# Summing attention weights over keys: accumulating DMAs in place of TensorE products and VectorE pair sums, with new scheduling priorities

## The chip, the cores and the metric

One core of one Trainium2 chip. The metric is device microseconds of one execution of the whole program. Every run quoted here was in the fast state. TensorE's granted clock is given as a share of full speed.

## The reference, cut to what matters

Sixteen graphs of 1024 nodes with 256 features share one sparse adjacency matrix. Each passes three graph-attention layers and then one layer of masked 8-head attention with a feed-forward part, all in fp32. The change concerns the attention layer:

```python
x, adj                                            # (16, 1024, 256), (1024, 1024)
for layer in (L0, L1, L2):                        # graph attention with 4, 1 and 1 heads
    x = x + layer(relu(layernorm(x)), adj, W, a)
h = relu(layernorm(x))
q, k, v = split(h @ w_qkv)                        # 8 heads of 32
scores = einsum('fnhd,fmhd->fhnm', q, k) / sqrt(32)
attn = softmax(where(adj > 0, scores, -1e9), -1)  # <- numerators and denominators
t = einsum('fhnm,fmhd->fnhd', attn, v)
h = layernorm(h + t); h = layernorm(h + ffn(h))
out = x + h                                       # the last residual; its x is loaded into the tile xr
```

## The kernel before

The kernel doesn't emit instructions where they are written. It records them, with a duration for each, and a list scheduler puts them into one fixed order per engine. Several batches are in flight, each an offset stream of priorities: a piece of work has as its key the batch number plus a position inside the stage, and of the work that is ready the smallest key goes first.

```python
class Record:
    def schedule(self):
        ...
            if x.key is None:
                x.key = base + span * x.pos / max(total, 1e-9)
        ...
            if x.moved:                               # a DMA: x.moved us of transfer
                queue[e] = max(at + 0.2, queue[e]) + x.moved
                x.pass_on = queue[e] + LANDING - (at + us)
```

`e` is the issuing engine: the model has one line of transfers for SyncE, another for GpSimd, and each moves at its own full pace. That will matter.

One attention layer has 32 steps: 2 groups of heads x 2 halves of the queries x 8 blocks of keys. I call the eight steps of one group and half a run. A step makes two tiles of masked exponentials (`pas`, 128 x 1024 each), multiplies them with the values on TensorE (a "quad": four column-tiled matmuls, one for each head, for two tiles), and needs their sum over keys, the denominator, by a quad against ones.

```python
def paired(g, hf):
    return g == 1 or hf == 1          # three runs of four
...
pe((1 + both) * 0.855, lambda: value(m, both), ...)   # both: also weights x ones
if not both and jt % 2:               # a quad on the sum of two steps
    pe(0.855, lambda: quad(accs[g, hf][1], ..., lambda r: ones, ...), ...)
...                                   # (cut: scores, exps, mask multiplies)
if paired(g, hf) and jt % 2:
    sums[n] = [r_sums.new() for _ in range(2)]
    for ss, p0, p1 in zip(sums[n], pas[n - 1], pas[n]):
        dve(tt_us(2 * HALF), lambda: nc.vector.tensor_add(ss.t, p0.t, p1.t), [ss], [p0, p1])
```

So one run in four multiplies every step by ones (8 quads), and three runs add pairs on VectorE and multiply those (4 quads each). The end of a batch matters too, because its transfers are what will suffer; `xr` has two buffers:

```python
def back(hf):
    for it in (hf * TH, hf * TH + 2):
        xr = r_xr.new()
        dma(1.15, lambda: nc.sync.dma_start(xr.t, x3.t[:, it : it + 2, :]), [xr(0), xr(1)], [x3(hf)])
        dve(tt_us(2 * C), lambda: nc.vector.tensor_add(xr.t, xr.t, rows["c2"]...), ...)
        ...                           # (cut: transposes, layer norm, scale, shift)
        dma(0.65, lambda: nc.sync.dma_start(out[b]...[:, it : it + 2, :], xr.t), [], [xr(0), xr(1)])
```

Of the kernel before, what the change touches and what calls it, by code (L numbers as in the profile page):

```python
# [17 lines left out]
ALU = mybir.AluOpType  # L18
# [96 lines left out]


class Record:

# [5 lines left out]

    def stream(self, base, span):


        self.streams.append([base, span, 0.0])

# [32 lines left out]
    def schedule(self):  # L162
        for n, x in enumerate(self.work):
            x.n = n
            base, span, total = x.stream
            if x.key is None:
                x.key = base + span * x.pos / max(total, 1e-9)
            x.left = len(x.before)
            for y in x.before:
                y.after.append(x)  # L170
# [43 lines left out]
        while True:  # L214
# [13 lines left out]
            us = x.us  # L228
# [24 lines left out]
LANDING = 2.5  # L253
BIAS = 0.516

# [18 lines left out]
def tt_us(n):  # L274
    return (n / 0.96 + 73) / 1000
# [17 lines left out]
def direct(ctx, tc, flag, x, adj, gat_w, gat_a, w_qkv, ln1_g, ln1_b, ln2_g, ln2_b, w1, b1, w2, b2, out):  # L293


    nc = tc.nc
# [7 lines left out]

    GATS = (0.0, 0.388), (0.388, 0.271), (0.659, 0.201)
    VALUES, STEPS, FEED = (1.132, 0.099), (1.231, 0.63), (2.355, 0.252)

# [84 lines left out]
    def dve(us, emit, w, r):  # L392
        rec.add("dve", us, emit, w, r)
# [196 lines left out]
    def setup():  # L590
        rec.stream(-3.0, 1.0)
        prepare(0)
        rec.stream(-0.9, 0.1)
        for it in range(NT):
            neighbours(it)
        rec.stream(-0.5, 0.3)
        prepare(1)
        prepare(2)
        dma(
            3.2,  # L600
            lambda: nc.sync.dma_start(wqkv_sb, w_qkv.rearrange("(t p) d -> p t d", p=P)),
            [b_qkv],
            [],
        )

        def load_feed():
            nc.sync.dma_start(w1_sb, w1.rearrange("(t p) d -> p t d", p=P))
            nc.sync.dma_start(w2_sb, w2.rearrange("(t p) d -> p t d", p=P))
            for n, ap in (("b1", b1), ("b2", b2), ("g1", ln1_g), ("c1", ln1_b)):
                nc.sync.dma_start(cols[n], ap.rearrange("(t p) -> p t", p=P))  # L610
            for n, ap in (("g2", ln2_g), ("c2", ln2_b)):
                nc.sync.dma_start(rows[n][:, 0, :], rows_on_all(ap, C))

        dma(5.0, load_feed, [b_feed], [], us=3.6)
# [346 lines left out]
    def attention(b, xt, b_mv, b_rstd):  # L961
        rec.stream(b + VALUES[0], VALUES[1])
        mv, rstd = b_mv.t, b_rstd.t
# [127 lines left out]

        def quad(ac, jt, of_head, columns, first, last):
            for r in range(HG):
# [7 lines left out]

        def value(n, both):

            g, hf, jt = steps[n]
            for ac in accs[g, hf][: 1 + both]:
                quad(
                    ac,
                    jt,
                    lambda r: pas[n][r // 2].t[:, r % 2, :],
                    lambda r: (  # L1110
                        ones
                        if ac is accs[g, hf][1]
                        else va.t[:, jt, (g * HG + r) * D3 : (g * HG + r + 1) * D3]
                    ),
                    jt == 0,
                    jt == NT - 1,
                )

        def paired(g, hf):

            return g == 1 or hf == 1

        rec.stream(b + STEPS[0], STEPS[1])
        GROUP = 2
        LAG = 2
        for n in range(len(steps) + LAG):
            m = n - LAG
            if m >= 0:
                g, hf, jt = steps[m]
                if jt == 0:  # L1130
                    accs[g, hf] = [r_bank.new(), r_bank.new()]
                both = not paired(g, hf)
                pe(
                    (1 + both) * 0.855,
                    lambda: value(m, both),
                    accs[g, hf],
                    pas[m] + [va(jt)],
                    ("col4", "col4"),
                )
                if not both and jt % 2:  # L1140
                    ss = sums[m]
                    pe(
                        0.855,
                        lambda: quad(
                            accs[g, hf][1],
                            jt,
                            lambda r: ss[r // 2].t[:, r % 2, :],
                            lambda r: ones,
                            jt == 1,
                            jt == NT - 1,  # L1150
# [56 lines left out]
            if n < len(steps):  # L1207
# [7 lines left out]
                for r0 in range(0, HG, GROUP):  # L1215
# [25 lines left out]
                    for r in range(r0, r0 + GROUP):  # L1241
# [9 lines left out]
                        if v:  # L1251
# [11 lines left out]
                            )  # L1263
                if paired(g, hf) and jt % 2:
                    sums[n] = [r_sums.new() for _ in range(2)]
                    for ss, p0, p1 in zip(sums[n], pas[n - 1], pas[n]):
                        dve(
                            tt_us(2 * HALF),
                            lambda: nc.vector.tensor_add(ss.t, p0.t, p1.t),  # L1269
                            [ss],  # L1270
                            [p0, p1],
                        )
        watch(b_rec, b_rec.t, 1)
# [178 lines left out]
    def batch(b):  # L1452
        xt, b_mv, b_rstd, x3 = Halves(r_xt), r_mv.new(), r_rstd.new(), r_x3.new()
        x_b = x[b].rearrange("(t p) c -> p t c", p=P)
        rec.stream(b, 0.0)
        for hf in range(2):
# [10 lines left out]
        for l in range(3):  # L1467
            rec.stream(b + GATS[l][0], GATS[l][1])
            gat(xt, b_mv, b_rstd, l)
# [8 lines left out]
        hn = attention(b, xt, b_mv, b_rstd)  # L1478
        rec.stream(b + FEED[0], FEED[1])
        feed(b, x3, hn)  # L1480
# [616 lines left out]
```

## Time and profile before

| | before |
|---|---|
| time, median of 4 runs | 4244.05 us (4240.61 to 4247.3) |
| TensorE / VectorE / ScalarE busy | 98% / 88% / 54% |
| DMA engines busy (the plain transfers' queue) | 22% |
| granted clock | 0.995 |
| denominator quads on TensorE | 320 (128 on weights, 192 on pair sums) |
| pair sums on VectorE | 384 |

How to read it: TensorE sets the time. The prediction below shows the lines that say so.

### The profile page before, as it was taken

To read this page: it belongs to the slowest core of one execution; us is meant where nothing else is said; L and a number is where in the kernel's file an instruction comes from. 1 tells how busy PE (TensorE), PEld (TensorE's weight loads), DVE (VectorE), ACT (ScalarE), POOL (GpSimd) and SP (SyncE) were. 2 spreads that over 40 slices of the span, in tenths; PEclk is the share of its full clock that TensorE was granted. 3 is DMA by queue.
4 is the path that set the end of the run, shared out by engine and by line. 5 is a ranking of instruction groups with operands and counts; after the bars stand their busy time and mean duration, and the time that the engine had idled before them with its cause. 6 is when DMAs were issued, how large, how long until landed. Compare 5 with 4: busy or idle time off the path is not lost.

```text
span 4234.8 us, 68471 instructions
## 1 busy us (share of the span) xinstructions
PE 4144.4 (98%) x24738; PEld 2385.9 (56%) x24738; DVE 3713.0 (88%) x6786; ACT 2307.1 (54%) x5041; POOL 351.7 (8%) x391
## 2 busy tenths in 40 slices
PE   7999999999999999999999999999999999999997
PEld 3746466564655646556464665646556465564642
DVE  7589898997989889898998989989898898988977
ACT  2445555554655645556555555656556455565564
POOL 0000010010100100001000100101001000010000
PEclk9999999999999999999999999999999999999998
DMA  3121222212222122221212222122212222212131
GB/s 103 50 66 36 76 66 66 56 46 70 68 75 53 50 66 61 81 63 56 60 48 75 66 66 56 50 66 71 76 52 60 56 60 81 64 52 60 47 82 39
DMA packets 180682, 263.82 MB, mean 62 GB/s; under 512 B 41328, under 2 KB 76400, under 8 KB 180336
## 3 DMA queue, kind: packets, MB, share of 16 engines
q1 hardware_dynamic: 180336, 259.36, 22.2%
q8 instruction: 198, 3.24, 0.3%
q14 instruction: 148, 1.21, 0.1%
HBM read 91.03 MB, written 33.95 MB: 30 GB/s over the span
## 4 chain that ended last, share of the span: by engine, by line
PE 73%; DVE 12%; ACT 7%; issue 3%; DMA 3%; POOL 2%; SPq 1%; DVEq 0%; ACTq 0%; POOLq 0%
PE bank L787 19%; PE bank L1094 12%; PE bank L861 9%; PE sc L1221 9%; PE bank L1327 5%; PE bank L871 5%; PE bank L663 4%; PE bank L460 4%; PE sc L1010 4%; DVE pa L1254 3%; DVE pt L760 2%; POOL rstd L412 2%; ACT hn L431 2%; ACT hna L431 2%; PE sc L1046 2%
## 5 line engine op out<-in xcount | busy, mean ns | idle before, releaser
L1245 ACT ACTIVATE pa<-sc 128x512 f32<-128x512 f32 x2048 | 1093.7, 608 | 610.3 <-PE sc L1221 524.7
L1254 DVE TENSOR_TENSOR pa<-pa,mask 128x1024 f32<-128x1024 f32 x1024 | 1220.2, 1215 | 48.5 <-ACT pa L1245 48.4
L760 DVE SCALAR_TENSOR_TENSOR pt<-row,e,mask 128x512 f32<-128x512 f32 x1536 | 1054.9, 744 | 90.7 <-DMA row<-rd 55.8
L787 PE MATMUL bank<-qb,pt 128*128 128x257 f32 x4096 | 940.9, 382 | 1.0 <-DVE pt L760 0.5
L787 PEld LDWEIGHTS bank<-qb,pt 128*128 128x128 f32 x4096 | 767.7, 190 | 197.5 <-ACT pa L1245 40.0
L1221 PE MATMUL sc<-qs,ks 128*128 128x512 f32 x2048 | 682.0, 446 | 2.9 <-ACT pa L1245 2.1
L1094 PE MATMUL bank<-pa,va 128*32 128x512 f32 x4096 | 533.0, 597 | 3.6 <-DVE pa L1254 3.2
L861 PE MATMUL bank<-pt,qb 128*32 128x512 f32 x4096 | 515.4, 595 | 7.3 <-DVE pt L760 6.7
L1221 PEld LDWEIGHTS sc<-qs,ks 128*128 128x128 f32 x2048 | 363.6, 188 | 237.1 <-ACT pa L1245 93.7
L1269 DVE TENSOR_TENSOR sums<-pa,pa 128x1024 f32<-128x1024 f32 x384 | 457.0, 1214 | 0.3 <-PE bank L1094 0.2
L663 PE MATMUL bank<-w_aug,hT 128*128 128x259 f32 (+1 forms) x1536 | 374.3, 388 | 4.3 <-ACT e L674 3.6
L815 ACT ACTIVATE ex<-bank,rec 128x256 f32<-128x256 f32 x256 | 122.1, 477 | 437.5 <-DVE rec L807 396.1
L663 PEld LDWEIGHTS bank<-w_aug,hT 128*128 128x128 f32 x1536 | 286.2, 191 | 74.0 <-issue 12.8
L412 POOL TENSOR_TENSOR rstd<-rstd,neg_half 128x4 f32<-128x4 f32 x160 | 203.1, 1272 | 1468.6 <-DVE rstd L409 1417.4
L861 PEld LDWEIGHTS bank<-pt,qb 128*32 128x32 f32 x4096 | 127.1, 109 | 310.0 <-issue 214.5
L871 PE MATMUL bank<-pt,e 128*32 128x512 f32 x2048 | 292.1, 592 | 0.0
L1094 PEld LDWEIGHTS bank<-pa,va 128*32 128x32 f32 x4096 | 116.2, 109 | 267.7 <-issue 208.7
L1010 PE MATMUL sc<-hTa,wqkv_sb 128*128 128x512 f32 x512 | 240.1, 596 | 4.6 <-ACT hTa L995 4.6
L431 ACT ACTIVATE hn<-xt,mv,rstd 128x256 f32<-128x256 f32 x384 | 206.3, 601 | 40.4 <-DVE mv L421 39.6
L892 ACT COPY ot<-bank 128x512 f32<-128x512 f32 x128 | 74.8, 586 | 257.7 <-PE bank L861 215.3
L1094 PE MATMUL bank<-sums,ones 128*32 128x512 f32 x1536 | 208.0, 596 | 0.8
L403 DVE BATCH_NORM_STATS2 stg<-xt 128x6 f32<-128x256 f32 x512 | 205.4, 414 | 3.2
(107 smaller groups left out, 3993.7 us busy)
## 6 DMA issues: line engine op xcount, KB each, us to landing
row<-rd SPq DMA_DIRECT2D x192, 256.0 KB
ks<-hi SPq DMA_DIRECT2D x512, 64.0 KB
ks<-lo SPq DMA_DIRECT2D x512, 64.0 KB
qs<-hi SPq DMA_DIRECT2D x512, 64.0 KB
qs<-lo SPq DMA_DIRECT2D x512, 64.0 KB
xt<-in_x_dram SPq DMA_DIRECT2D x32, 512.0 KB
x<-xt SPq DMA_DIRECT2D x32, 512.0 KB
xr<-x SPq DMA_DIRECT2D x64, 256.0 KB
```

What stands on the lines that cost most here:

```text
L431: lambda: nc.scalar.activation(dst, src, func, bias=bias, scale=scale),
L663: nc.tensor.matmul(g.t[:, : C + 3 * H], hT.t[:, ct, k * P : (k + 1) * P], w_aug[l][:, ct, :], start=ct == 0, stop=ct == CT - 1,)
L760: lambda: nc.vector.scalar_tensor_tensor(pt.t, row.t, e3[:, 2, jt // TH, h, jt % TH : jt % TH + 1], mask[:, jt, hf * HALF : (hf + 1) * HAL ...
L787: nc.tensor.matmul(g.t[:, : D + 1], pts[jt].t[:, k * P : (k + 1) * P], qb[:, jt, 0, :], start=jt == 0, stop=jt == NT - 1,)
L861: nc.tensor.matmul(g.t[u * D + d : u * D + d + D3, :], qb[:, j, h + u, d : d + D3], pts[u][j - jt].t, start=j == 0, stop=j == NT - 1,)
L871: nc.tensor.matmul(gd.t[c : c + D3, :], one(jt + k, h + u).to_broadcast([P, D3]), pts[u][k].t, start=jt == 0, stop=jt == NT - 2,)
L1010: nc.tensor.matmul(sc.t, wqkv_sb[:, ct, c0 : c0 + P], hT.t[:, ct, hf * HALF : (hf + 1) * HALF], start=ct == 0, stop=ct == CT - 1,)
L1094: nc.tensor.matmul(ac.t[r * D3 : (r + 1) * D3, :], columns(r), of_head(r), start=first, stop=last,)
L1221: nc.tensor.matmul(scs[r - r0].t, ks.t[:, r, jt * P : (jt + 1) * P].bitcast(F32R), q.t[:, r, :].bitcast(F32R), start=True, stop=True,)
L1245: lambda: nc.scalar.activation(pt.t[:, v, :], sc.t, AF.Exp, scale=1.0 / math.sqrt(D3)),
L1254: lambda: nc.vector.tensor_mul(pt.t, pt.t, mask[:, jt : jt + 1, i0 : i0 + HALF].to_broadcast([P, 2, HALF]),),
L1269: lambda: nc.vector.tensor_add(ss.t, p0.t, p1.t),
```

## The change

Intent: take work from the two fullest engines and give it to the DMA engines, which are three quarters idle. In every run VectorE adds the first two steps into a tile, six DMAs per tile add the other steps onto it, and one quad per run multiplies the result by ones. Priorities get five knots per stage in place of a straight line, an offset for ScalarE's and VectorE's work (`LEAD`) and a stronger bias against changes of TensorE's mode. The diff, cut to its core:

```diff
+def priority(x):
+    base, knots, total, lead = x.stream
+    at = x.pos / max(total, 1e-9) * (len(knots) - 1)
+    k = max(0, min(int(at), len(knots) - 2))
+    key = base + knots[k] + (knots[k + 1] - knots[k]) * (at - k)
+    return round(key - (LEAD.get(x.engine, 0.0) if lead else 0.0), 6)
...
-BIAS = 0.516
+BIAS = 0.676
+LEAD = {"act": -2.125, "dve": 1.391}
...
-    GATS = (0.0, 0.388), (0.388, 0.271), (0.659, 0.201)
-    VALUES, STEPS, FEED = (1.132, 0.099), (1.231, 0.63), (2.355, 0.252)
+    GATS = ((-0.005, 0.055, 0.156, 0.243, 0.247), ...)
+    VALUES = (1.165, 1.186, 1.197, 1.164, 1.074)
+    STEPS = (1.085, 1.251, 1.421, 1.645, 1.91)
+    FEED = (2.225, 2.388, 2.391, 2.491, 2.389)
...
+        RUN = 8
...
+                if jt % RUN == 1:
+                    sums[g, hf] = [r_sums.new() for _ in range(2)]
+                    for ss, p0, p1 in zip(sums[g, hf], pas[m - 1], pas[m]):
+                        dve(tt_us(2 * HALF), lambda: nc.vector.tensor_add(ss.t, p0.t, p1.t), [ss], [p0, p1])
+                elif jt % RUN:
+                    for ss, pt in zip(sums[g, hf], pas[m]):
+                        dma(2.8, lambda: nc.gpsimd.dma_start(ss.t, pt.t, accum_op=ALU.add),
+                            [ss], [pt], us=0.88, engine="pool")
...
-                if not both and jt % 2:
-                    ss = sums[m]
+                if jt % RUN == RUN - 1:
+                    ss = sums[g, hf]
                     pe(0.855, ...quad against ones...)
...
-                if paired(g, hf) and jt % 2:
-                    ...pair sums on VectorE...
```

More of the change, by code (lines that the diff above doesn't have):

```diff
@@ L123, in __init__, with stream @@
         self.streams = []
-    def stream(self, base, span):
-        self.streams.append([base, span, 0.0])
+    def stream(self, base, knots, lead=True):
+        self.streams.append([base, knots, 0.0, lead])
     def add(self, engine, us, emit, w=(), r=(), modes=("full", "full"), key=None, moved=0.0):
@@ L164, in schedule @@
             x.n = n
-            base, span, total = x.stream
             if x.key is None:
-                x.key = base + span * x.pos / max(total, 1e-9)
+                x.key = priority(x)
             x.left = len(x.before)
@@ L303, in direct @@
     HG = P // D3
-    GATS = (0.0, 0.388), (0.388, 0.271), (0.659, 0.201)
-    VALUES, STEPS, FEED = (1.132, 0.099), (1.231, 0.63), (2.355, 0.252)
+    GATS = (
+        (-0.005, 0.055, 0.156, 0.243, 0.247),
+        (0.285, 0.416, 0.523, 0.588, 0.743),
+        (-0.041, 0.393, 0.575, 0.619, 0.945),
+    )
+    VALUES = (1.165, 1.186, 1.197, 1.164, 1.074)
+    STEPS = (1.085, 1.251, 1.421, 1.645, 1.91)
+    FEED = (2.225, 2.388, 2.391, 2.491, 2.389)
     const = ctx.enter_context(tc.tile_pool(name="const", bufs=1))
@@ L590, in setup @@
     def setup():
-        rec.stream(-3.0, 1.0)
+        rec.stream(-3.0, (0.0, 1.0), False)
         prepare(0)
-        rec.stream(-0.9, 0.1)
+        rec.stream(-0.9, (0.0, 0.1), False)
         for it in range(NT):
             neighbours(it)
-        rec.stream(-0.5, 0.3)
+        rec.stream(-0.5, (0.0, 0.3), False)
         prepare(1)
@@ L961, in attention @@
     def attention(b, xt, b_mv, b_rstd):
-        rec.stream(b + VALUES[0], VALUES[1])
+        rec.stream(b, VALUES)
         mv, rstd = b_mv.t, b_rstd.t
@@ L1090, in attention, with quad @@
         pas, accs, sums = {}, {}, {}
-        def quad(ac, jt, of_head, columns, first, last):
+        def quad(ac, of_head, columns, first, last):
             for r in range(HG):
@@ L1100, in quad @@
                 )
-        def value(n, both):
-            g, hf, jt = steps[n]
-            for ac in accs[g, hf][: 1 + both]:
-                quad(
-                    ac,
-                    jt,
-                    lambda r: pas[n][r // 2].t[:, r % 2, :],
-                    lambda r: (
-                        ones
-                        if ac is accs[g, hf][1]
-                        else va.t[:, jt, (g * HG + r) * D3 : (g * HG + r + 1) * D3]
-                    ),
-                    jt == 0,
-                    jt == NT - 1,
-                )
-        def paired(g, hf):
-            return g == 1 or hf == 1
-        rec.stream(b + STEPS[0], STEPS[1])
+        RUN = 8
+        rec.stream(b, STEPS)
         GROUP = 2
@@ L1131, in attention @@
                     accs[g, hf] = [r_bank.new(), r_bank.new()]
-                both = not paired(g, hf)
-                pe(
-                    (1 + both) * 0.855,
-                    lambda: value(m, both),
-                    accs[g, hf],
+                if jt % RUN == 1:
+                    sums[g, hf] = [r_sums.new() for _ in range(2)]
+                    for ss, p0, p1 in zip(sums[g, hf], pas[m - 1], pas[m]):
+                        dve(
+                            tt_us(2 * HALF),
+                            lambda: nc.vector.tensor_add(ss.t, p0.t, p1.t),
+                            [ss],
+                            [p0, p1],
+                        )
+                elif jt % RUN:
+                    for ss, pt in zip(sums[g, hf], pas[m]):
+                        dma(
+                            2.8,
+                            lambda: nc.gpsimd.dma_start(ss.t, pt.t, accum_op=ALU.add),
+                            [ss],
+                            [pt],
+                            us=0.88,
+                            engine="pool",
+                        )
+                pe(
+                    0.855,
+                    lambda: quad(
+                        accs[g, hf][0],
+                        lambda r: pas[m][r // 2].t[:, r % 2, :],
+                        lambda r: va.t[:, jt, (g * HG + r) * D3 : (g * HG + r + 1) * D3],
+                        jt == 0,
+                        jt == NT - 1,
+                    ),
+                    [accs[g, hf][0]],
                     pas[m] + [va(jt)],
@@ L1145, in attention @@
                             accs[g, hf][1],
-                            jt,
                             lambda r: ss[r // 2].t[:, r % 2, :],
                             lambda r: ones,
-                            jt == 1,
+                            jt == RUN - 1,
                             jt == NT - 1,
@@ L1263, in attention @@
                             )
-                if paired(g, hf) and jt % 2:
-                    sums[n] = [r_sums.new() for _ in range(2)]
-                    for ss, p0, p1 in zip(sums[n], pas[n - 1], pas[n]):
-                        dve(
-                            tt_us(2 * HALF),
-                            lambda: nc.vector.tensor_add(ss.t, p0.t, p1.t),
-                            [ss],
-                            [p0, p1],
-                        )
         watch(b_rec, b_rec.t, 1)
@@ L1454, in batch @@
         x_b = x[b].rearrange("(t p) c -> p t c", p=P)
-        rec.stream(b, 0.0)
+        rec.stream(b, (0.0, 0.0), False)
         for hf in range(2):
@@ L1467, in batch @@
         for l in range(3):
-            rec.stream(b + GATS[l][0], GATS[l][1])
+            rec.stream(b, GATS[l])
             gat(xt, b_mv, b_rstd, l)
@@ L1478, in batch @@
         hn = attention(b, xt, b_mv, b_rstd)
-        rec.stream(b + FEED[0], FEED[1])
+        rec.stream(b, FEED)
         feed(b, x3, hn)
```

## The prediction

> **What bounds the kernel now.** I read the page's engine shares first, then busy time by stretch, then the groups of instructions, then the chain that ended last, then the DMA part and the waits.
>
> ```profile
> PE 4144.4 (98%) x24738; PEld 2385.9 (56%) x24738; DVE 3713.0 (88%) x6786; ACT 2307.1 (54%) x5041; POOL 351.7 (8%) x391
> ...
> q1 hardware_dynamic: 180336, 259.36, 22.2%
> ```
>
> TensorE is busy 98% of the span, VectorE 88%, GpSimd 8%, the DMA engines 22%. A busy share can hide waiting, so I asked for stretches (columns: window, its length, busy us and instructions of PE, PEld, DVE, ACT and POOL, then TensorE clock, DMA share, GB/s):
>
> ```profile
> 0.00:100.00 100.00, 75.83 (x522) 34.20 (x526) 81.11 (x176) 28.52 (x57) 4.62 (x12) 0.93 0.33 109
> ...
> 400.00:4000.00 3600.00, 3573.69 (x21602) 2077.61 (x21602) 3224.59 (x5886) 2003.46 (x4399) 309.14 (x336) 1.00 0.23 62
> ...
> 4100.00:4235.00 135.00, 111.65 (x490) 41.26 (x488) 109.97 (x168) 64.29 (x120) 9.21 (x9) 0.92 0.20 52
> ```
>
> From 400 to 4000 us TensorE is idle for 3600 - 3573.69 = 26 us, 0.7%. The kernel interleaves the streams of several batches, and there the schedule leaves almost nothing to take from waits: only removed TensorE time shortens it. The idle time is at the two ends. Does "busy" mean "at its pace"? The chain of waits in order of time answers (start us, us, what):
>
> ```profile
> 1536.33 1.14 PE sc L1221 x4
> 1537.47 1.85 PE bank L861 x16
> ...
> 1540.18 1.72 PE bank L861 x16
> ...
> 1542.76 3.44 PE bank L1094 x32
> ```
>
> Link follows link without a hole, and 32 instructions of L1094 take 3.44 us. Such a quad (four matmuls on four column groups) is 8 instructions, so a quad advances the chain by 0.86 us. That is the pace I use; the 1.04 us that a lone quad shows as busy in the timeline includes an end that overlaps its successor. The groups that the change touches (busy us, mean ns of one | idle before):
>
> ```profile
> L1254 DVE TENSOR_TENSOR pa<-pa,mask 128x1024 f32<-128x1024 f32 x1024 | 1220.2, 1215 | 48.5 <-ACT pa L1245 48.4
> ...
> L1269 DVE TENSOR_TENSOR sums<-pa,pa 128x1024 f32<-128x1024 f32 x384 | 457.0, 1214 | 0.3 <-PE bank L1094 0.2
> ...
> L1094 PE MATMUL bank<-sums,ones 128*32 128x512 f32 x1536 | 208.0, 596 | 0.8
> ```
>
> VectorE adds pairs of weight tiles (384 adds of 1.214 us) and TensorE sums over keys by quads against ones: 1536 / 8 = 192 on pair sums. A further group, the weights against ones directly, has 1024 instructions in the full list of groups: 128 quads, from the quarter of the attention that isn't paired.
>
> **What the Trainium skill says.** (1) "DMA: Bandwidth & Descriptors", section "SWDGE vs HWDGE vs iDMA": an accumulating DMA can only be issued from GpSimd, whose cores build its descriptors; plain ones can go from SyncE. The trace has no such DMA: the 22.2% are all of the hardware kind, so its cost isn't measured here. (2) The same page, "Anatomy of one DMA — SWDGE (gpsimd) path", gives about 2 us fixed per DMA beside the data, and "Rules for kernel authors" says that an accumulate must wait for the earlier DMA on the same bytes. So six additions into one tile are a chain. No run here shows that yet. (3) "Collectives: The Full Stack", "The bandwidth ceiling: the fold count and why AG ≠ RS ≠ AR": adding in the DMA datapath costs not the addition but a second read, measured there at 1.93 times a copy. That is for collectives; I take it over as an estimate. (4) "TensorEngine Tiling (Array Packing)", "Key Properties": changing the tiling mode drains TensorE. The trace agrees: in the chain above the column-tiled L861 takes 1.85 us after another mode and 1.72 us after its own, so 0.13 us for that change.
>
> **The change part by part.**
>
> *TensorE.* Before: 128 + 192 = 320 denominator quads. After: one per eight steps, 4 per batch, 64 in 16 batches. Removed: 256 quads at 0.86 us = 220 us. All of it stood on the path, since TensorE has 0.7% idle. The value quads, scores and the graph layers are unchanged.
>
> *VectorE.* Before 384 adds. After: one add for each of 2 tiles in 4 runs of eight steps, 8 per batch, 128 in all. Removed: 256 at 1.214 us = 311 us. Off the path in the steady part, so worth no time directly. It matters as room: VectorE goes to 3713 - 311 = 3402 us, and 3402 over a span of some 4030 us is 84%, below its present 88%. TensorE goes to about 3924 of 4030, 97%. So VectorE doesn't become the bound.
>
> *DMA and GpSimd.* New: 6 steps x 2 tiles x 4 runs x 16 batches = 768 accumulating DMAs of 128 x 1024 fp32 = 512 KB, 403 MB. The trace's list of DMA packets has 5,120 of 4,096 B (the row length of these tiles) with a mean of 162.7 ns; a 512 KB transfer has 128 of them, 8 per engine, so a plain copy takes 1.30 us of all 16 engines. Twice that for the second read: 2.6 us, an estimate from this trace and the skill's 1.93. The scheduler's own table in the diff books 2.8 us. So 768 x 2.6 to 2.8 = 2.0 to 2.15 ms; with the present 0.222 x 4235 = 940 us the DMA engines go to 3.0 to 3.1 ms of 4030, about 75%. Busy, not full. GpSimd: the diff books 0.88 us an issue, 676 us; with its 352 us about a quarter of the span.
>
> Does the chain of additions keep up? A step adds two tiles, 5.2 to 5.6 us of transfer. In a steady batch, from the first to the last exp in a run of eight steps takes about 58, 58, 39 and 47 us (start times of L1245), 4.9 to 7.3 us per step, and only six of eight need DMAs: 31 to 34 us of transfer in 39 us at the tightest. It fits, without much spare. The new priority knots move and stretch the attention steps (from 0.63 to 0.825 of a batch period between first and last knot), which I read as room made for just this.
>
> *The ends.* The last batch has no other stream beside it. Its four runs take about 34, 31, 29 and 28 us. The same chain needs 6 x 5.2 = 31 us of transfer, about 2 us for a last landing and 2 to 3 us for the first add and the closing quad: 36 us. So 36 - 30.5 = 5.5 us per run, 22 us for four, given back at the tail.
>
> *Priorities and mode changes.* In the order of start times TensorE leaves the column-tiled mode 368 times. The bias against changing mode rises from 0.516 to 0.676, and the odd lone denominator quads vanish. The two changes around a column-tiled block cost at most about 0.34 us by the chain (0.13 us on entering, 1.14 against 0.93 us for the scores after it), so all of them about 125 us; a tenth fewer gives 12 us. The knots have nothing else to gain where TensorE is already 99.3% busy.
>
> *Sum.* 4246 - 220 - 12 + 22 (tail) + about 10 for accumulations that arrive late in the steady part (my choice: less than a fifth of a microsecond per run) = 4046; I say **4045 us**, 4.7% faster.
>
> **The rivals.**
>
> *The DMA chain becomes the bound.* If an accumulation takes 4 us of all engines rather than 2.7, a step needs 8 us, a run 48 us and a batch 192 us of transfer besides the 58 us (22% of some 257 us) that the other DMAs use: 250 us against the planned 243. The ring of six weight tiles (three steps) then stays full, exp waits, TensorE's fixed order waits for it. For: the order is static, the chain is serial, the model of the queue books each issuing engine by itself and so ignores that SyncE's transfers share the 16 engines. Against: 1.30 us for a plain copy, measured. It would make about 4150 to 4350 us.
>
> *A new wait takes part of the gain.* Rows for the graph layers come by DMA, and VectorE already waits for them:
>
> ```profile
> DVE pt L760 <- DMA row<-rd: 55.8, 31, 8.1
> ```
>
> With 75% of the DMA time taken, rows and the key and query stacks land later; GpSimd also computes the inverse deviations (L412, 1.27 us each) and stands in order behind an accumulation that waits. For: these are latencies ahead of a layer's start. Against: VectorE gets 311 us of slack and several streams are there to fill in. One or two us per run of eight steps, 64 runs, gives 4100 to 4170 us.
>
> *The gain is full or better.* If the tail is hidden by the new priorities and mode changes fall by a quarter (31 us), 4246 - 220 - 31 = 3995, and with a shorter start 3980.
>
> **Range and chances.** The 220 us are counted instructions at a measured pace; the doubt is what DMA waits give back. The full-gain case sets the low end at 3975, a loss of some 85 us against my estimate the high end at 4130. Faster by over 2% means below 4161: 115 us or 52% of the removed quads must be lost before it fails. That needs the first rival in part or the second at its worst: 0.12. Slower than 4331 needs the first rival in full: 0.02. Faster 0.86.
>
> **What would show it.** Right: 512 instructions of sums against ones, none of weights against ones, 128 adds on VectorE at 1.21 us, TensorE busy near 3920 us and still over 98% busy between 400 and 4000 us; DMA share near 75%; TensorE's waits short. Each step wrong: packets of the accumulating queue well over 330 ns (DMA estimate); "exp waits for DMA sums" or TensorE waiting on weight tiles in the steady part (chain too slow); VectorE's wait on rows well over 56 us (contention); last four runs not near 36 us (tail); mode changes not below 368 (bias). The prediction is wrong if the engines' time per accumulation is over about 3.5 us, or if GpSimd's order holds the layers' starts back.

## The result, and the profile after

| | before | after |
|---|---|---|
| time, median of 4 runs each | 4244.05 us | 4372.4 us (4364.45 to 4376.53) |
| ratio | 1 | 1.030 (95%: 1.0281 to 1.032) |
| granted clock | 0.995 | 0.966 |
| from the first exp of one batch to that of the next, mean of 14 | 256.5 us | 261.4 us |
| from the first exp of the last batch to the end | 175 us | 239 us |

The change is 3% slower. Ratios are the mean time of one kernel's fast runs over that of the other's of the same rounds, so not quite the ratio of the medians quoted. The last two rows split the loss: 14 x 4.9 = 69 us in the steady part and 64 us in the tail.

Engine shares and DMA queues of the page after (busy us, share, instructions; packets, MB, share of 16 engines):

```profile
PE 4026.2 (92%) x22690; PEld 2355.8 (54%) x22690; DVE 3457.6 (79%) x6530; ACT 2360.7 (54%) x5041; POOL 993.8 (23%) x1159
...
q0 software_dynamic: 110592, 402.70, 48.7%
q1 hardware_dynamic: 180336, 259.36, 21.1%
```

TensorE has 2048 matmuls fewer, as the change says (256 quads of 8), and yet only 118 us less busy time, and it is now idle for 8% of the span. The DMA engines work 70% of it. The steady stretch of after (same columns as in the prediction):

```profile
400.00:4000.00 3600.00, 3383.49 (x19470) 2003.73 (x19469) 2944.51 (x5564) 2011.71 (x4308) 851.35 (x988) 0.98 0.73 157
```

TensorE was idle 26 us in this stretch before; now 3600 - 3383.49 = 216.5 us. What does it wait for? The longest of its matmul waits in this stretch (total us, times, longest):

```profile
PE bank L677 <- DVE yT L1374: 130.2, 14, 10.5
```

Fourteen times, once for each steady batch, some 9 us each, 130 of the 216 us: TensorE's next item is a product of a graph layer (L677) whose PSUM bank is held until VectorE has read the feed-forward result of another batch into `yT`. Why does VectorE come late? Its group that loses most, after and then before (busy us, mean ns | idle before it, what ended it):

```profile
L1394 DVE TENSOR_TENSOR xr<-xr,row_c 128x512 f32<-128x512 f32 x64 | 43.5, 679 | 171.1 <-DMA xr<-x 171.1
```

```profile
L1385 DVE TENSOR_TENSOR xr<-xr,row_c 128x512 f32<-128x512 f32 x64 | 43.5, 679 | 17.6 <-DMA xr<-x 17.6
```

VectorE's fixed order puts this small addition ahead of `yT`, and it waits for a load of `xr` that SyncE issues. One of the fourteen, in order of time in after (start us, us, engine line operation, idle before):

```profile
2124.53 3.36 SPq L1045 DMA_DIRECT2D ks<-hi  x4
2126.88 0.48 DVE L1439 SCALAR_TENSOR_TENSOR xr<-fz,rstdz,xr 128x256 f32<-128x256 f32 x1
2127.98 4.69 SPq L1045 DMA_DIRECT2D ks<-lo  x4
2132.72 3.97 SPq L1045 DMA_DIRECT2D ks<-hi  x4
2136.74 4.88 SPq L1045 DMA_DIRECT2D ks<-lo  x4
...
2141.65 1.91 PE L677 MATMUL bank<-w_aug,hT 128*128 128x259 f32 x8
...
2141.71 1.03 SPq L1447 DMA_DIRECT2D out_dram<-xr  x1
...
2147.84 0.33 SPq L1388 DMA_DIRECT2D xr<-x  x1
...
2152.05 0.69 DVE L1394 TENSOR_TENSOR xr<-xr,row_c 128x512 f32<-128x512 f32 x1 [10.02 <-DMA xr<-x]
2152.66 0.74 DVE L1374 SCALAR_TENSOR_TENSOR yT<-bank,col_b,yT 128x512 f32<-128x512 f32 x1
...
2153.46 3.74 PE L677 MATMUL bank<-w_aug,hT 128*128 128x259 f32 x8 [9.89 <-DVE yT L1374]
```

The same spot of a batch in before:

```profile
1864.35 0.39 SPq L1438 DMA_DIRECT2D out_dram<-xr  x1
...
1866.52 0.32 SPq L1379 DMA_DIRECT2D xr<-x  x1
...
1869.48 0.69 DVE L1385 TENSOR_TENSOR xr<-xr,row_c 128x512 f32<-128x512 f32 x1 [0.60 <-DMA xr<-x]
```

Read it downward. VectorE completes the output tile at 2127.4 us (L1439, the second of the tile's two), but SyncE's order has sixteen slices of the key stack first, the last four of them in 4.88 us, and the output transfer is issued 14.4 us later, at 2141.7. Over the steady batches the first output of a batch waited 14.3 us in this way, 0.3 us in before. (I paired completed tiles and outputs by their order.) The next load of `xr` goes into a buffer that this transfer must have left. In before it was issued 2.2 us after the output transfer, now 6.1 us after. From the issue of the load to the addition that waits for it went 4.2 us; it was 3.0. VectorE stands 10 us, TensorE 9.9. And when TensorE goes on, the same eight matmuls of L677 that took 1.91 us before the gap take 3.74 us. Windows around the gap (the last three columns are granted clock, DMA share, GB/s):

```profile
2130.00:2143.60 13.60, 13.40 (x58) 7.19 (x56) 10.15 (x15) 10.81 (x23) 5.38 (x6) 1.00 1.03 207
2143.60:2153.50 9.90, 0.04 (x1) 0.04 (x1) 1.45 (x3) 0.65 (x2) 1.72 (x2) 0.66 1.04 223
2153.50:2157.20 3.70, 3.70 (x10) 2.87 (x11) 2.76 (x4) 0.65 (x2) 0.00 (x0) 0.53 0.46 132
```

Before and in the gap the DMA engines are full: a mean share of 73% hides stretches of 100%. The clock falls to half 3.2 us into the gap and stays there until 3.5 us after it. Shorter gaps sometimes do it too. In after's timeline of TensorE:

```profile
2077.68 0.66 PE L474 MATMUL bank<-ident,hna 128*128 128x128 f32 x4 [2.16 <-DVE rec L931]
...
2078.90 1.94 PE L1108 MATMUL bank<-pa,va 128*32 128x512 f32 x8
```

A gap of 2.16 us, and the next quad takes 1.94 us in place of 1.04; the clock record shows 0.50 from 2078.5 to 2081.9. The Trainium skill, "TensorE: Matmul & The Clock Gate", section "Why this matters for your kernels", says to leave no idle gaps over about 3 us between matmul bursts, or the clock goes back to half. The trace agrees that idle gaps are followed by a halved clock, but shows no sharp limit: in after's steady stretch all 14 gaps over 5 us met a clock of 0.50, and of 14 gaps between 2 and 3 us eight did (the shortest 2.16 us) and six didn't (the longest 2.51 us). Before had no such gap: its longest was 1.6 us, and its clock stood at 1.0 without a break, both from 117 to 4180 us.

This isn't the only way in which the bytes reach TensorE. GpSimd and ScalarE wait for the accumulations themselves:

```profile
POOL sums L1140 <- DMA sums<-pa: 378.4, 152, 5.0
ACT pa L1263 <- DMA sums<-pa: 142.7, 111, 10.7
```

GpSimd can't issue the next addition into a tile before the last has landed, and what stands behind in its order, such as the inverse deviations, waits with it: VectorE's wait for those went from 54 us in before to 113. An exp waits for a weight tile that an addition still reads. And in the chain that ended last the accumulations have the largest share of all transfers, 7% of the span.

### The profile page after: what moved, and what is told of

Same layout as the page of the kernel before. It is cut to its first block, busy times and chain, and to the rows that moved or that the text cites. A ratio compares the mean times of both kernels' runs of the same rounds, so it can differ in the third digit from the quotient of the medians.

```text
span 4366.9 us, 66311 instructions
## 1 busy us (share of the span) xinstructions
PE 4026.2 (92%) x22690; PEld 2355.8 (54%) x22690; DVE 3457.6 (79%) x6530; ACT 2360.7 (54%) x5041; POOL 993.8 (23%) x1159
## 3 DMA queue, kind: packets, MB, share of 16 engines
q1 hardware_dynamic: 180336, 259.36, 21.1%
## 4 chain that ended last, share of the span: by engine, by line
PE 43%; DVE 22%; DMA 17%; issue 6%; SPq 6%; ACT 4%; POOL 2%; DVEq 0%; ACTq 0%; POOLq 0%
PE bank L801 11%; DVE pt L774 8%; DMA sums<-pa 7%; DVE pa L1272 6%; SPq L1045 6%; PE bank L1108 5%; PE bank L677 5%; PE bank L875 5%; PE sc L1239 4%; DMA row<-rd 3%; PE bank L474 3%; PE bank L885 2%; DMA out_dram<-xr 2%; PE sc L1024 2%; PE bank L1336 2%
## 5 line engine op out<-in xcount | busy, mean ns | idle before, releaser
L1140 POOL DMA_DIRECT2D sums<-pa x768 | 671.6, 876 | 2346.6 <-DVE pa L1272 744.9
L1239 PE MATMUL sc<-qs,ks 128*128 128x512 f32 x2048 | 721.4, 458 | 46.4 <-ACT pa L1263 26.3
L1108 PE MATMUL bank<-pa,va 128*32 128x512 f32 x4096 | 549.9, 612 | 24.4 <-DVE pa L1272 21.7
L677 PE MATMUL bank<-w_aug,hT 128*128 128x259 f32 (+1 forms) x1536 | 397.9, 409 | 137.7 <-DVE yT L1374 130.2
L677 PEld LDWEIGHTS bank<-w_aug,hT 128*128 128x128 f32 x1536 | 302.7, 202 | 231.6 <-DVE yT L1374 135.9
L708 DVE TENSOR_TENSOR qb<-bank,e 128x256 f32<-128x256 f32 x128 | 53.1, 423 | 177.6 <-ACT e L688 177.6
L688 ACT ACTIVATE e<-bank 128x3 f32<-128x3 f32 (+1 forms) x384 | 68.5, 185 | 207.0 <-PE bank L677 204.4
```

Source lines behind the costliest of these rows:

```text
L677: nc.tensor.matmul(g.t[:, : C + 3 * H], hT.t[:, ct, k * P : (k + 1) * P], w_aug[l][:, ct, :], start=ct == 0, stop=ct == CT - 1,)
L1108: nc.tensor.matmul(ac.t[r * D3 : (r + 1) * D3, :], columns(r), of_head(r), start=first, stop=last,)
L1140: lambda: nc.gpsimd.dma_start(ss.t, pt.t, accum_op=ALU.add),
L1239: nc.tensor.matmul(scs[r - r0].t, ks.t[:, r, jt * P : (jt + 1) * P].bitcast(F32R), q.t[:, r, :].bitcast(F32R), start=True, stop=True,)
```

## The experiments

**Theories.** A: the accumulations take the 16 DMA engines that SyncE's transfers need, these land late, and the fixed order, planned with one line of transfers for each issuing engine, stands on them. B: the new priorities are at fault, not the accumulations. C: the chain of accumulations is too slow, or holds its weight tiles too long. D: GpSimd's 768 issues, or its waiting to issue them, hold its other work back.

A word on the order: the scheduler's own model can be run without a chip. It expects the end at 4259 us for before and 4031 us for after; before is 15 us faster than that, after 341 us slower. Whatever goes wrong is something that it doesn't know.

All of them at a glance. Idle is TensorE's, in the stretch from 400 to 4000 us; DMA share is of the same stretch:

| kernel | median us | ratio to before (95%) | idle us | DMA share |
|---|---|---|---|---|
| before | 4244 | 1 | 26 | 0.23 |
| after | 4372 | 1.030 (1.028, 1.032) | 217 | 0.73 |
| thin64 | 4012 | 0.945 (0.944, 0.947) | 51 | 0.36 |
| half256 | 4093 | 0.964 (0.962, 0.966) | 90 | 0.54 |
| sum_only | 4654 | 1.096 (1.094, 1.098) | 260 | 0.67 |
| prio_only | 4311 | 1.016 (1.014, 1.017) | 28 | 0.23 |
| xr3 | 4395 | 1.036 (1.034, 1.038) | 224 | 0.72 |
| out_act | 4340 | 1.023 (1.021, 1.026) | 199 | 0.73 |
| shared | 4325 | 1.020 (1.018, 1.021) | 122 | 0.74 |
| junk | 4651 | 1.097 (1.095, 1.099) | 261 | 0.64 |
| tuned2 | 4275 | 1.007 (1.005, 1.010) | 119 | 0.75 |
| tuned8444 | 4234 | 0.998 (0.997, 1.000) | 67 | 0.62 |
| tuned8242 | 4204 | 0.992 (0.990, 0.993) | 27 | 0.44 |
| tunedpairs | 4254 | 1.003 (1.002, 1.004) | 10 | 0.23 |

### The bytes of the accumulations alone: thin64 and half256

Same instructions, same order, same number of accumulations; only each one adds fewer bytes (64 KB or 256 KB of 512). The result is wrong on purpose (relative error 0.15 and 0.17), and a lower bound of 0.001 keeps the reciprocals finite (one small VectorE instruction, 64 times).

```diff
-    lambda: nc.gpsimd.dma_start(ss.t, pt.t, accum_op=ALU.add),
+    lambda: nc.gpsimd.dma_start(ss.t[:, 0, :128], pt.t[:, 0, :128], accum_op=ALU.add),  # thin64
+    lambda: nc.gpsimd.dma_start(ss.t[:, 0, :], pt.t[:, 0, :], accum_op=ALU.add),        # half256
```

> The changed kernel with the same order and the same 768 accumulating DMAs, but each adds only 128 of a row's 1024 columns (64 KB in place of 512 KB). Wrong result on purpose; a maximum against 0.001 before the reciprocal (64 small instructions) keeps it finite. Contention theory (the 16 DMA engines, 49% taken by the accumulations, deliver SyncE's transfers two to three times later than the fixed order allows, TensorE stands about 10 us per batch on them and its clock then halves): the wait of L677 on yT (130 us in 14 times) falls below 20 us, TensorE idle below 60 us between 400 and 4000 us, clock back to 0.99, time 4030 to 4100 us. Rival, GpSimd's order (inverse deviations stand behind accumulations, 0.88 us an issue): the issues and the order stay, so 4300 us or more. Rival, the new priorities alone: nothing of them changes, 4330 us or more.

> As the run with 64 KB, but each accumulation adds 512 of 1024 columns (256 KB). Wrong result on purpose. Contention theory: the DMA share falls from about 70% to about 46%, latencies of SyncE's transfers most of the way back, so more than half of the loss returns: 4060 to 4200 us, wait of L677 on yT 0 to 70 us. Rivals (GpSimd's order, priorities): unchanged, 4330 us or more.

Measured: 4012.1 us, 18 us below the range expected, and 4092.75 us, within it. The steady stretch of thin64, with TensorE's idle time down to 51 us at full clock:

```profile
400.00:4000.00 3600.00, 3549.46 (x20605) 2103.39 (x20603) 3149.19 (x5977) 2165.49 (x4626) 957.00 (x1077) 1.00 0.36 79
```

and VectorE's wait for `xr`, 171.1 us in after:

```profile
DVE xr L1397 <- DMA xr<-x: 27.7, 18, 3.0
```

What follows: the bytes cost 4372 - 4012 = 360 us. GpSimd's issues by themselves don't make this loss, since it issues as often here. But fewer bytes relieve two things at once: the shared engines, and each accumulation, which lands after a median of 2.3 us (3.6 us in half256) in place of 5.5. The waits for accumulations shrink with it:

```profile
POOL sums L1140 <- DMA sums<-pa: 61.1, 55, 3.3
ACT pa L1266 <- DMA sums<-pa: 6.8, 2, 6.5
```

So this run can't tell A from C, or from GpSimd's waiting in D. The loss isn't in proportion: the first 192 KB added to each accumulation cost 81 us, the other 256 KB 280 us. That fits a resource that gets full in stretches; it fits a chain that outgrows its steps as well. As for SyncE's line: the order is the same, and the first output of a batch waits 7.9 us here against 14.3. So about half of that delay is the new order's, and half comes with the bytes.

### One half of the change each: sum_only and prio_only

`sum_only` has the new summing under the old priorities (straight lines written as two knots, no `LEAD`, `BIAS` 0.516); `prio_only` the reverse.

```diff
+    BIAS = 0.516; LEAD = {}; STEPS = (1.231, 1.861); ...   # sum_only, against after
```

```diff
+    BIAS = 0.676; LEAD = {"act": -2.125, "dve": 1.391}; STEPS = (1.085, ..., 1.91); ...   # prio_only, against before
```

> The new way of summing with the priorities of before (two-knot lines with the old numbers, no lead, bias 0.516). Contention theory: the same bytes share the DMA engines, the order is another but no more planned for it: 4250 to 4450 us, TensorE idle 100 to 350 us between 400 and 4000 us. Rival, the new priorities are the cause: 4020 to 4120 us, TensorE 99% busy.

> The new priorities with the old way of summing (pairs on VectorE, no accumulating DMA). Contention theory: no accumulation, so DMA share near 22%, TensorE work as before (4144 us busy), the clock near 0.99 and no wait of 10 us for yT; the knots were made for less VectorE and TensorE work, so somewhat over the kernel before: 4240 to 4330 us. Rival, the new priorities are the cause of the loss: their loss stays though the 220 us of TensorE work are back, 4450 us or more.

Measured: 4654.36 (worse than expected) and 4311.34 us. B falls as the main cause. The new priorities cost 67 us with the old summing, which they weren't made for, and the scheduler's model knows of this: it plans 4318 us. With the accumulations they are 282 us better than the old ones, of which the model plans 198 (4229 against 4031). What the model doesn't know is the loss that comes with the accumulations: 425 us over plan here, 341 in after. In `sum_only` the accumulations' own lateness weighs most: they have the largest share of the chain that ended last, 25% of the span.

### The suspected wait at the spot itself: xr3 and out_act

Two ways to take away what the load of `xr` waits for: a third buffer, or the output transfers issued from ScalarE so that they don't stand in SyncE's line.

```diff
-    r_xr = ring("xr", 2, [2, C])
+    r_xr = ring("xr", 3, [2, C])                   # xr3
```

```diff
-    lambda: nc.sync.dma_start(out[b]..., xr.t), [], [xr(0), xr(1)],
+    lambda: nc.scalar.dma_start(out[b]..., xr.t), [], [xr(0), xr(1)], engine="act",   # out_act
```

> The changed kernel with three buffers in place of two for the tile xr (the last residual), so that its load waits for the output transfer of three tiles before, not two. The bytes of all transfers stay. If the 10 us per batch come from SyncE's line (output transfer landing, then the xr load, then rows, while VectorE stands on xr and TensorE on VectorE): the wait of L677 on yT falls from 130 us to below 50 us and the time to 4220 to 4320 us, above the 4093 us of half the bytes, since other transfers stay late. If instead the chain of additions itself is what holds (weight tiles kept by late accumulations): no change, 4350 us or more, with exp waiting for the accumulations as before (143 us).

> The changed kernel with the output transfers (out from xr) issued by ScalarE, so that they don't stand in SyncE's line behind key and query transfers; the bytes stay. SyncE's line as the cause: output leaves up to 5 us sooner, the wait of L677 on yT falls to below 80 us, 4260 to 4340 us. Chain of additions as the cause: no change, 4350 us or more.

Measured: 4394.81 and 4339.57 us. The third buffer does not help; TensorE's wait on `yT` is 136 us there. By what was expected, this outcome spoke for the chain of additions, but it doesn't decide, because the wait that the buffer was to remove is still there: the chain of `xr3` shows SyncE issuing key slices one after the other, and then an output transfer of 5.6 us and a load of 4.1 us all the same. (The scheduler also makes another order, so this isn't a pure removal.) Taking the output out of SyncE's line, with the planned end unchanged, takes away 33 us and brings the wait on `yT` to 96 us (below 80 was expected). SyncE's line is a part of the cause, about a tenth of the 360 us, not all of it.

### Contention without a chain of additions: junk

The kernel before, in its own order, plus 768 plain transfers of 1 MB (the mask, to spare memory) issued by GpSimd, paced by the attention steps. Nothing waits for the transfers, and nothing is summed; the scheduler's order of all other work is the same. But each transfer follows a one-element copy that reads a weight tile, so a tile is held until GpSimd has come to its copy. The result is right.

```diff
+    if m >= 0 and jt % 8 > 1:
+        for u in range(2):
+            jk = r_junk.new()
+            dma(0.0, lambda: (nc.gpsimd.tensor_copy(pace, pas[m][u].t[:, 0, :1]),
+                              nc.gpsimd.dma_start(jk.t, mask)),
+                [jk], [b_mask, pas[m][u]], us=0.0, engine="pool")
```

> The kernel before, same order on all engines, with 768 plain transfers of 1 MB added that nothing waits for (the mask to spare tiles in HBM, issued by GpSimd in the six steps in which the changed kernel accumulates, each after a one-element copy that waits for that step's weights). About 2 ms of all 16 DMA engines, as the accumulations take, but no chain of additions, no weight tile kept for them, no fewer denominator quads. Contention theory: SyncE's transfers come late against an order not planned for it, TensorE idle 80 to 300 us between 400 and 4000 us in place of 26, DMA share 65 to 75%, time 4320 to 4500 us. If the chain of additions was the cause: 4235 to 4270 us, TensorE idle as before.

Measured: 4650.8 us, larger than expected. TensorE's steady stretch and its two longest matmul waits there:

```profile
400.00:4000.00 3600.00, 3338.54 (x19626) 1911.86 (x19626) 2930.90 (x5341) 1823.78 (x3983) 1142.48 (x1516) 0.97 0.64 233
```

```profile
PE sc L1237 <- DVE lo L1024: 116.3, 25, 7.1
PE bank L665 <- ACT qb L687: 93.8, 12, 9.2
```

The pacing copies did hold exps up (ScalarE's wait over the whole run):

```profile
ACT pa L1261 <- POOL pace L1140: 104.0, 15, 9.3
```

What follows: transfers on another engine's queue, that no one waits for, together with their pacing copies cost some 400 us, with the same signs (idle TensorE, clock 0.966, VectorE's wait for `xr` at 229 us). A loss of this size needs no chain of additions. How much of it is the copies' was not measured apart; the longest of their waits, at 665 us, began with VectorE standing on a load of `xr`. For after itself C isn't excluded as a part: TensorE's own wait on accumulations was only 8 us, but ScalarE's was 143 and GpSimd's 378, and they are 7% of its chain. Why junk is worse than after at a lower DMA share stays open; it moves twice the bytes, to memory outside the core, under an order planned with no such load at all.

### Tell the scheduler: shared and tuned2

One line of transfers in the model for all issuing engines; then knots, bias and leads searched again on the host for the earliest planned end under that model (4225 us for `shared`, 4141 for `tuned2`).

```diff
-    queue[e] = max(at + 0.2, queue[e]) + x.moved
-    x.pass_on = queue[e] + LANDING - (at + us)
+    queue["dma"] = max(at + 0.2, queue["dma"]) + x.moved
+    x.pass_on = queue["dma"] + LANDING - (at + us)
```

> The changed kernel with one line of its scheduler altered: the transfers that SyncE and GpSimd issue fill one common queue in its model of time, not one queue for each, so that the fixed order knows of late transfers. Same instructions, same bytes, same priorities, another order. Contention theory (order planned for transfers that come too early): fewer waits, 4230 to 4340 us, clock over 0.975. If the order doesn't matter and the bandwidth alone bounds: 4350 us or more.

> The changed kernel with the scheduler's common queue for all transfers, and the knots, bias and leads searched anew under it (annealing on the planned end: 4141 us, after 4225 us with the knots as they were, which ran in 4325 us). Contention theory: an order made for late transfers gets most of the removed TensorE work back: 4190 to 4270 us. If bandwidth bounds whatever the order: 4300 us or more.

Measured: 4324.66 and 4274.74 us, the second just outside what was expected. `shared` misses its plan by 100 us where after missed by 341. In `shared` the wait that began this is mostly gone:

```profile
PE bank L677 <- DVE yT L1374: 30.6, 13, 5.2
```

So an order that reckons with one shared line stands less (122 us against 217), at a clock of 0.983; this supports A. ScalarE's wait for accumulations is not gone but longer, 263 us. And the shared line doesn't make the change pay: at a share of 0.75 some 120 us of idle time remain in both.

### Fewer accumulations: tuned8444, tuned8242, tunedpairs

If the DMA engines are too full, the balance can be moved: long sums where there is room, short ones elsewhere. `RUNS` gives the length of a sum in each of a batch's four runs. (8, 4, 4, 4) makes 576 accumulations, 112 quads and 224 adds; (8, 2, 4, 2) makes 320, 176 and 352. `tunedpairs` has the old summing with the shared line and its own search, to tell the gain of the search from that of the sums.

```diff
-    RUN = 8
+    RUNS = (8, 2, 4, 2)               # tuned8242
...
+    RUN = RUNS[2 * g + hf]
+    # own knots: GATS (-0.543, -0.54, -0.26, -0.042, 0.376), (0.326, 0.562, 0.551, 0.653, 1.024), (-0.111, 0.157, 0.239, 0.149, 0.467);
+    # VALUES (0.973, 0.878, 1.201, 1.257, 1.324), STEPS (1.253, 1.475, 1.546, 1.708, 2.038), FEED (2.151, 2.443, 2.443, 2.504, 2.62);
+    # BIAS 0.738, LEAD act 5.525, dve 2.336
```

> As the run before it, but the last three of a batch's four runs of eight steps sum in fours (VectorE adds the second step to the first, two steps by DMA, a denominator quad each four steps): 576 accumulations in place of 768, 112 denominator quads in place of 64 (41 us more TensorE work), 224 VectorE adds in place of 128; its own knots, planned end 4128 us. Fewer bytes and shorter chains: 4150 to 4240 us, faster than the kernel before, DMA share near 60%. If only bytes counted (between the runs with half and all of them, 4093 and 4325 us, plus 41 us): about 4250 us.

> Fewer bytes still: of a batch's four runs of eight steps the first sums all eight (six steps by DMA), the third in fours (two of four by DMA), the second and fourth in pairs on VectorE without DMA. 320 accumulations in place of 768, 176 denominator quads (144 or 124 us fewer than before), 352 VectorE adds; common queue in the scheduler, own knots, planned end 4165 us. DMA share near 43%. The plan was missed by 106 us at 61% and by 133 us at 72%, and met within 15 us at 22%: 4170 to 4225 us, faster than the kernel before by 0.5 to 1.5%.

> Control for the run beside it: the old way of summing (no accumulation by DMA) with the common queue and knots searched anew in the same way, planned end 4223 us where the kernel before has 4259. If the search of knots alone explains a gain of the run beside it, this one gains as much; if the removed quads do, this stays within 4205 to 4250 us.

Measured: 4233.57 and 4204.11 us, as expected, and 4253.77 us, 4 us over its range. The steady stretch of tuned8242:

```profile
400.00:4000.00 3600.00, 3572.57 (x20958) 2083.57 (x20958) 3254.41 (x5982) 2082.43 (x4497) 730.19 (x624) 1.00 0.44 104
```

TensorE is as full as before (27 us idle) at full clock, with 144 quads fewer. This version beats both kernels: 0.85% under before, 4% under after. The search alone gives nothing (1.003), so the gain comes with the sums. It is a small gain, under the 2% that I would call faster.

## Why the prediction was wrong

Point by point, by its own steps.

- **The removed TensorE work: right.** 256 quads and a gain of 220 us on the path, plus 12 for mode changes. Without the bytes (thin64) the kernel takes 232 us less than before, and TensorE is busy 3912 us; predicted was near 3920.
- **The mode changes: wrong, small.** TensorE leaves the column-tiled mode 374 times, not fewer than 368. That the total agrees with 232 us all the same is in part luck: these 12 us didn't come, thin64's tail is 10 us longer than before's, and something else makes up for it.
- **An accumulation's cost: right.** Its 4,096 B packets have a mean of 343.7 ns, eight on each engine: 2.75 us of all engines, predicted 2.6 to 2.8. The share of the steady stretch is 0.73, predicted 75%. "Busy, not full" was true of the mean alone; the windows at the stall show 1.03 and 1.04.
- **The first rival, the chain: wrong in its size, right in part.** It asked for 4 us of all engines an accumulation; it is 2.75. But the check "It fits" reckoned with transfer time alone and left the fixed time of about 2 us, which the prediction had quoted, to the tail. From issue to landing an accumulation took 5.5 us, and the sign that the prediction set for a slow chain, exps waiting for sums, did show (143 us, 84 of them in the steady stretch). The rival's "for" named a right flaw, too: the model of the queue ignores that SyncE's transfers share the engines. I tied this flaw to a rival that the 1.30 us of a copy spoke against, and dropped it with that rival.
- **"About 10 for accumulations that arrive late in the steady part": the step that failed.** It was a choice and not a sum, too small for the accumulations' own lateness, and it had nothing for what they do to all other transfers. The second rival did ask for that, naming late rows and stacks and GpSimd standing behind an accumulation, but was sized at one or two us per run, with VectorE's slack and the other streams as the reason. Its sign came: VectorE's wait on rows is 99 us, 56 in before. The slack didn't help, because in the fixed order VectorE stood 10 us on `xr` with other work behind it. Measured against before, TensorE's steady idle time rose by 216.5 - 26.3 = 190 us, over some 56 runs 3.4 us each. The Trainium skill, "DMA: Bandwidth & Descriptors", section "Issuing engines are not separate DMA queues", says that transfers run on the same 16 engines and interleave whoever started them; the trace agrees (the load behind an output transfer was issued 2.2 us after it then, 6.1 now). I had quoted that page for other points and given this one no number.
- **No term for the clock: missing.** The instructions are the same in thin64 and after, but TensorE is busy 4026.2 - 3912.1 = 114 us longer in after. I put this down to the clock, 0.966 against 0.993: 3912 x 0.993 / 0.966 = 4021. Of the 356 us between the two profiled spans, 242 are idle time and 114 are longer busy time, so each microsecond of standing came with about another half.
- **The tail: right sign, too small.** Predicted +22 us, measured 239 - 175 = 64. The last four runs take 38, 53, 48 and 39 us, predicted 36 each. In thin64 the tail is 185 us, so 54 of the 64 are the bytes. There the chain does show; ScalarE's wait from 4128 us to the end:

```profile
ACT pa L1263 <- DMA sums<-pa: 46.1, 22, 10.7
```

- **The sum.** 4045 predicted, 4372 measured. Against thin64 (4012) the bytes add 14 x (261.4 - 240.8) = 288 us in the steady part, 54 in the tail, and 13 before the second batch's first exp (468 against 455 us): 355 of the 356 us between the two profiled spans.

What the runs show: the bytes of the accumulations make the loss, other transfers of about the same DMA time (with their pacing copies) make one of that size without any sums, and a plan with one shared line removes part of it. One part is traced to its end: late loads of `xr`, 130 us of TensorE's 216 idle us. What stays open: how after's whole loss, and the difference between tuned2 (4275) and thin64 (4012), split into SyncE's slower issues, transfers that wait on full engines, and accumulations that hold weight tiles and GpSimd's order. No experiment here separates them; one that shortens the waits for accumulations and keeps the bytes would. One thing the queue totals exclude: the packets of the plain transfers didn't get slower themselves (21.1% of 4367 us in after, 22.2% of 4235 in before), so a plain transfer that lands later has waited before its packets or between them.

## What to carry to other kernels

A DMA that replaces compute isn't free because the engines are mostly idle on average: look at the share in short windows, and ask which small latency-bound transfers will stand behind it, and which fixed order stands on those. If a schedule comes from a model, give the model one shared line of transfers, and move only as much work as leaves the engines well below full in every stretch (here 0.44 paid, 0.62 was level, 0.73 lost; the orders and the work removed differ too, so this is no threshold). To size such a change, keep its instructions and shrink its bytes: the thin version shows the gain without the cost of the bytes. It doesn't say which wait makes the cost.

## What the Trainium skill lacked or had wrong

- "DMA: Bandwidth & Descriptors": it has no cost for an accumulating DMA between tiles on the core. Here one of 512 KB with 4 KB rows took 2.75 us of all 16 engines, its packets 343.7 ns against 164.9 ns for plain packets of the same size (2.08 times), and 5.5 us from issue to landing (4.4 to 10.0), with 0.88 us on GpSimd to issue it. The 1.93 of "Collectives: The Full Stack" was a good estimate.
- "DMA: Bandwidth & Descriptors", "Issuing engines are not separate DMA queues": it says that transfers interleave, but not how much a small transfer suffers. Here the next load could follow a 256 KB output transfer after 6.1 us in place of 2.2, and where engines were full (share 1.03) four 64 KB transfers took SyncE 4.9 us to issue. The median for four is 2.5 us in both kernels, but 70 of 408 fours took over 4 us, against none of 427 in before.
- "TensorE: Matmul & The Clock Gate", "Why this matters for your kernels": the limit of about 3 us is too lenient for this case. A gap of 2.16 us was followed by 3.4 us at a clock of 0.50, and so were eight of 14 gaps between 2 and 3 us; the other six were not.
- No page says what late transfers do to an order of instructions that is fixed ahead: here TensorE's idle time in the steady stretch went from 26 to 217 us, and between thin64 and after 242 us of standing came with 114 us of longer busy time.
